# Pairs 2 and 3 get their stacked halves of x from ScalarE and VectorE; the table's scaling moves to GpSimd; new order up to pair 5

## The chip, the cores and the metric

One NeuronCore of a Trainium2 chip runs the kernel. Its engines are TensorE (PE; PEld is its weight load), VectorE (DVE), ScalarE (ACT), GpSimd (POOL) and SyncE (SP), which only issues DMAs here. The metric is the device time of one execution in microseconds, the median over runs.

## The reference

`x` is (64, 64, 1024) float32: 64 batches of 64 channels by 1024. Each batch picks one of 16 weight matrices of 64 by 64, and what comes out goes through a 1024 by 1024 linear layer whose weights are packed 6-bit integers:

```python
W = weights[condition]                      # (64, 64, 64)
h = jnp.einsum('bct,bcd->bdt', x, W)
w = (unpacked.astype(jnp.float32) - zero_point) * scale   # 6-bit fields of qweight
y = jnp.einsum('bsk,nk->bsn', h, w) + bias
return x + y
```

## The kernel before

The 64 batches are worked on as 32 pairs, two pairs to a group (g = p // 2). A pair's x lies on 128 partitions: batch one's channels on the lower 64 (`LO`), batch two's on the upper 64 (`HI`).

**Arithmetic.** PE multiplies in float16, so each float32 operand is cut into a high and a low half. For x, `magnitudes` (ScalarE) sums absolute values, `bounds` (one tiny matmul) spreads the sums, `scales` or `scales_in_full` (DVE) make powers of two of them, `split_1` (ScalarE) writes the scaled high half `hf` and the sums of x, and `split_2` (DVE) the low half `lf`. Stage 1 needs a batch's high half and low half stacked on 128 partitions as one operand `xa`; `stack_high` and `stack_low` do that with four DMAs on SP's queue.

**Stage 1** (`stage1`): 32 matmuls of 64 columns make `ph`, 1024 columns in PSUM, one buffer for all pairs; `stage1_high` (ScalarE) and `stage1_low` (DVE) cut it into `hh` and `hl`. **Stage 2** (`products`): 8 tiles of the contraction, `hh` and `hl`, two PSUM banks: 32 matmuls of 512 columns into `po`, of which even and odd pairs have one buffer each. `stage2_bank(p, n)` is one bank of a pair, `stage2_tiles` some tiles of both.

**Output.** `po` is scaled on DVE (`scale_out`), x is added (`accumulate`) and stored. What the zero points and the bias add has been put onto x by GpSimd (`zero_points`, `add_bias`). For pairs 0 to 3 the result is kept as `res` (`early_minus`, `early_res`) and put onto x later (`early_add`).

**The weights' table** is scaled (`weights_scaled`), cut into halves (`weights_high`, `weights_low`), and each pair's two matrices are selected from it: by GpSimd copies for pairs 2 to 7, by DMAs on SP from pair 8 on. Pairs 0 and 1 take another way: `early_stage1` multiplies x in float32 with unscaled weights, and `early_bounds`, `early_scales`, `early_high`, `early_low` cut the result.

**Order.** The order of instructions on each engine is the order in which the code is written; nothing reorders it. Each engine runs its own list and waits on semaphores, so an instruction that waits holds up all behind it on its engine, and the same holds for DMAs on SP. Up to pair 3 the steps stand one by one (L540 to L678); from pair 3 on `window(p)` issues stage 1 of pair p + 1, the tails of pair p - 1, the preparation of the next groups, and stage 2 of pair p. A run of dummy matmuls (`WARM`) comes first.

Of the kernel before, what the change touches and what calls it, by code (L numbers as in the profile page):

```python
# [8 lines left out]
F32 = mybir.dt.float32  # L9
# [20 lines left out]
def adaln_ffn(ctx: ExitStack, tc: tile.TileContext, x, cond, cw, qw, ws, wz, bias, out):  # L30
# [6 lines left out]
    NG = NP // 2  # L37
    KT = T // P
    LO, HI = slice(0, C), slice(C, P)
    WARM = 36  # L40

    xf = x.rearrange("(i j) c t -> (j c) i t", j=2)
    of = out.rearrange("(i j) c t -> (j c) i t", j=2)
# [6 lines left out]
    unpacking = ExitStack()  # L50
    qp = unpacking.enter_context(tc.tile_pool(name="qp", bufs=3))
    ps_s = ctx.enter_context(tc.tile_pool(name="ps_s", bufs=2, space=bass.MemoryType.PSUM))
    ps_o = [ctx.enter_context(tc.tile_pool(name="ps_a", bufs=1, space=bass.MemoryType.PSUM))]

    ctx.enter_context(tc.manual_schedule())
    ctx.enter_context(nc.allow_low_precision("bounds of magnitudes alone"))
# [10 lines left out]
    def load_x(g):  # L67
        xts[g] = xp.tile([P, 2, T], F32, name="xt")
        nc.sync.dma_start(xts[g], xf[:, 2 * g : 2 * g + 2, :])
# [26 lines left out]
    load_pair(3)  # L96
    nc.sync.dma_start(scb, ws.rearrange("n o -> (n o)").partition_broadcast(P))
    load_x(2)


    dummy = const.tile([P, P], BF, name="dummy")
# [79 lines left out]
        powers(tmp["pw"], wup, wdn)  # L181

    def weights_scaled():
        nc.vector.tensor_tensor(wsc, w32, wdn.unsqueeze(2).to_broadcast([P, NK, D]), ALU.mult)

    def weights_high():
        nc.scalar.copy(tab[:, :, 0, :], wsc)
# [100 lines left out]
    def split_2(g, i, ts_=ALL):  # L288

        nc.vector.scalar_tensor_tensor(  # L290
            st[g]["lf"][:, i, ts_],
            xts[g][:, i, ts_],
            st[g]["down"][:, i : i + 1],
            st[g]["hf"][:, i, ts_],
            ALU.mult,
            ALU.subtract,
        )

    def stack_high(g, sl=BOTH, ts_=ALL):
# [84 lines left out]
    def early_bounds(p, parts):  # L384
        pl = ps_s.tile([P, 2], F32, name="pl", tag="s")
        for n in range(parts):
            nc.tensor.matmul(pl, lhsT=all_ones, rhs=pb[:, p, n, :], start=(n == 0), stop=(n == parts - 1))
        tmp["pl"] = pl
# [8 lines left out]
    def early_stage1(p, ph, kts=range(KT)):  # L397
        for kt in kts:
            nc.tensor.matmul(  # L399
                ph[:, kt % ph.shape[1], :, :], lhsT=xts[0][:, p, ts(kt, P)], rhs=wbd[:, p, :], start=True, stop=True  # L400
            )
# [50 lines left out]

    def stage1(p):
        g, i = divmod(p, 2)
        ph = ps_o[2].tile([P, KT, 2, D], F32, name="ph")
        for kt in range(KT):
            for j in range(2):
                for a in range(2):
                    nc.tensor.matmul(  # L459
                        ph[:, kt, j, :],  # L460
                        lhsT=st[g]["xa"][:, i, j, ts(kt, P)],
                        rhs=wsts[g][:, i, a, j, :],
                        start=(a == 0),
                        stop=(a == 1),
                    )
        return ph.rearrange("p k j d -> p k (j d)")
# [25 lines left out]

    def stage2_tiles(p, kts, ks=range(2)):
        if p not in pos:
            pos[p] = ps_o[p % 2].tile([P, N], F32, name="po", tag="po")
        products(pos[p], p, kts, ks, BANKS, BANKS)

    def stage2_bank(p, n, ks=range(2), kts=range(KT)):
        if p not in pos:
            pos[p] = ps_o[p % 2].tile([P, N], F32, name="po", tag="po")  # L500
        for k in ks:
            products(pos[p], p, kts, [k], [BANKS[n]], [BANKS[n]])

# [40 lines left out]
    early = ExitStack()  # L544
    ps_e = early.enter_context(tc.tile_pool(name="ps_e", bufs=2, space=bass.MemoryType.PSUM))
    ph0a, ph0b = [ps_e.tile([P, KT // 2, 2, D], F32, name="ph0") for _ in range(2)]
    ph1 = ps_e.tile([P, KT, 2, D], F32, name="ph1", bufs=1)
    HALF = [slice(0, T // 2), slice(T // 2, T)]
    early_select(0, 0, nc.gpsimd)
    early_select(0, 1, nc.scalar)  # L550
# [9 lines left out]
    early_rows(0, 0)  # L560
    early_rows(0, 1)
    early_stage1(0, ph0b, range(4, KT))
    early_bounds(0, 2)
    early_scales(0)
    early_high(0, ph0a, LOWER)
    early_high(0, ph0b, UPPER)
    early_weights(1)
    early_stage1(1, ph1)
    unpack(0)
    unpack(1)  # L570
    early_low(0, ph0a, LOWER)
# [8 lines left out]
    early_rows(1, 0)  # L580
    unpack(6, 2)
    early_sums(0)
    stage2_tiles(0, range(2, 4))
    weights_bounds()
    early_bounds(1, 1)
# [2 lines left out]
    weights_scaled()  # L588
    magnitudes(1, 0)
    early_high(1, ph1, slice(0, KT))  # L590
    stage2_tiles(0, range(4, 5))
    bounds(1, FIRST)
    scales(1, FIRST)
    stage2_tiles(0, range(5, 6))
    early_low(1, ph1, slice(0, KT))
    early.close()
    for n in ("b", "h"):
        ps_o.append(ctx.enter_context(tc.tile_pool(name="ps_" + n, bufs=1, space=bass.MemoryType.PSUM)))
    split_1(1, 0)
    stack_high(1, FIRST)  # L600
    weights_high()
    split_2(1, 0)
    stack_low(1, FIRST)
    load_pair(6)
    stage2_tiles(0, range(6, KT))
    early_feature_sums(0)
    weights_low()
    early_unscales(0)
    unpacking.close()
    late = ctx.enter_context(tc.tile_pool(name="late", bufs=1))  # L610
    for n in range(2, 8):
        select_pair(n, nc.gpsimd)
    magnitudes(1, 1)


    stage2_tiles(1, range(0, 4), [0])
    early_zero_points(0)
    stage2_tiles(1, range(0, 4), [1])
    bounds(1, SECOND)
    scales(1, SECOND)  # L620
    early_out(0)
    early_sums(1)
    split_1(1, 1)
    stack_high(1, SECOND)
    split_2(1, 1)
    stack_low(1, SECOND)
    load_pair(7)
    nc.sync.dma_start(bib, bias.partition_broadcast(P))
    stage2_tiles(1, range(4, 7))
    ph = stage1(2)  # L630
    magnitudes(2, 0)
    stage1_high(2, ph, LOWER)
    stage1_high(2, ph, UPPER)
    magnitudes(2, 1)
    stage2_tiles(1, range(7, KT))
    stage1_low(2, ph)
    early_unscales(1)
    weights_hot()


    stage2_bank(2, 0, [0])
    bounds(2)
    scales(2)
    sums_high(1)
    sums_low(1, nc.gpsimd)
    split_1(2, 0)
    stage2_bank(2, 0, [1], range(0, 6))
    weights_of_batches()
    stage2_bank(2, 0, [1], range(6, KT))
    early_feature_sums(1)  # L650
    early_zero_points(1)
    unscales(1)
    unscales(2)
    split_2(2, 0)
    stack_high(2, FIRST)
    stack_low(2, FIRST)
    feature_sums(1)
    unscale_sums(1)
    early_minus(1)
    ph = stage1(3)  # L660
    stage1_high(3, ph)
    stage1_low(3, ph)
    early_res(1)
    split_1(2, 1)
    sums_high(2)
    magnitudes(3, 0)
    magnitudes(3, 1)
    early_zero_points(2)
    stage2_bank(2, 1)
    sums_low(2, nc.vector)  # L670
    split_2(2, 1)
    stack_high(2, SECOND)
    stack_low(2, SECOND)
    nc.vector.tensor_tensor(zsc, zsb, scb, ALU.mult)
    load_x(4)
    early_zero_points(3)
    add_bias(4)
    add_bias(5)  # L678


    LATE = {5 + 2 * n: ((add_bias, early_add)[n % 2], n // 2) for n in range(8)}
# [1 line left out]
    def window(p):  # L683

        g, i = divmod(p, 2)
        if p + 1 < NP:
            ph = stage1(p + 1)
        if p == 3:

            stage2_bank(p, 0)  # L690
        if i == 1 and g + 2 < NG:
            bounds(g + 2)
        if i == 1 and g + 1 < NG:
            feature_sums(g + 1)
        if p - 1 < 4:
            early_out(p - 1)
        else:
            scale_out(p - 1)
        if i == 1 and g + 2 < NG:
            scales_in_full(g + 2)  # L700
        if i == 1 and g + 1 < NG:
            unscale_sums(g + 1)
        if p + 1 < NP:
            stage1_high(p + 1, ph)
        if p - 1 >= 4:
            accumulate(p - 1)
            store(p - 1)
        if p + 1 < NP:
            stage1_low(p + 1, ph)
        if i == 0:  # L710
            if g + 3 < NG:
                load_x(g + 3)
            if g + 1 < NG:
                sums_high(g + 1)
                sums_low(g + 1, nc.scalar)
            if g + 2 < NG:
                magnitudes(g + 2, 0)
                magnitudes(g + 2, 1)
            if g + 1 < NG:
                add_bias(p + 2)  # L720
                add_bias(p + 3)
            if g + 2 < NG:
                select(g + 2)
        else:
            if g + 2 < NG:
                for n in range(2):
                    split_1(g + 2, n)
                    split_2(g + 2, n)
                stack_high(g + 2)
                stack_low(g + 2)  # L730
            if g + 1 < NG:
                zero_points(p + 1)
                zero_points(p + 2)
        if p in LATE:

            what, n = LATE[p]
            what(n)
            if what is early_add:
                store(n)
        if p == 3:  # L740
            stage2_bank(p, 1)
        elif p < NP - 1:
            stage2(p)
# [2 lines left out]
        window(p)  # L746

    p = NP - 1
    for cols, pool, tag in ((slice(0, 512), ps_o[1], "po"), (slice(512, 768), ps_o[2], "ph"), (slice(768, N), ps_o[0], "po")):
        po = pool.tile([P, cols.stop - cols.start], F32, name="pe", tag=tag)  # L750
        products(po, p, range(KT), range(2), [cols], [slice(0, cols.stop - cols.start)])
        scale_out(p, cols, po)
        accumulate(p, cols, po)
        store(p, cols)
# [61 lines left out]
```

## Time and profile before

| what | us |
|---|---|
| median of three runs | 270.55 (270.04 to 270.96) |
| the profiled execution | 271.06 |
| its span | 269.3 |
| PE busy | 261.7 (97%) |
| DVE busy | 199.8 (74%) |
| POOL busy | 168.8 (63%) |
| ACT busy | 158.3 (59%) |
| DMA queue, share of 16 engines' span | 66.9% |
| granted PE clock | 0.999 |

"Span" is the time from the profile's first instruction to its last; the execution's own time is 1.8 us longer. In lines of a timeline the columns are start and duration in us, engine, source line, operation, the tiles written and read, partitions of each operand by shape, and the count; in square brackets stands how long the engine was idle before it and what ended that. In lines of the chain they are start, duration, and what the time went to; "issue" is time without a visible cause, "SPq" SP's issuing of a DMA. A line of the waits names the engine and line that waited, what for, the total in us, the times, and the longest. A matmul's duration overlaps the next one's, so its starts are more telling than its ends.

### The profile page before, as it was taken

To read this page: it belongs to the slowest core of one execution; us is meant where nothing else is said; L and a number is where in the kernel's file an instruction comes from. 1 tells how busy PE (TensorE), PEld (TensorE's weight loads), DVE (VectorE), ACT (ScalarE), POOL (GpSimd) and SP (SyncE) were. 2 spreads that over 40 slices of the span, in tenths; PEclk is the share of its full clock that TensorE was granted. 3 is DMA by queue.
4 is the path that set the end of the run, shared out by engine and by line. 5 is a ranking of instruction groups with operands and counts; after the bars stand their busy time and mean duration, and the time that the engine had idled before them with its cause. 6 is when DMAs were issued, how large, how long until landed. Compare 5 with 4: busy or idle time off the path is not lost.

```text
span 269.3 us, 5717 instructions
## 1 busy us (share of the span) xinstructions
PE 261.7 (97%) x2154; PEld 140.4 (52%) x2154; DVE 199.8 (74%) x271; ACT 158.3 (59%) x283; POOL 168.8 (63%) x96
## 2 busy tenths in 40 slices
PE   8999979999999999999999999999999999999993
PEld 7645535545555554555555455555455555545553
DVE  3897899585795959779595976959598695955543
ACT  3588888576655657666565765656676555634100
POOL 3004253949598695959969596995929386595100
PEclk9999999999999999999999999999999999999999
DMA  6997766957567696597956797677976764551112
GB/s 192 326 356 182 235 133 203 259 167 214 198 148 246 198 266 218 141 322 199 290 170 192 219 268 235 181 245 230 279 222 185 210 170 142 161 158 79 78 50 108
DMA packets 32476, 54.39 MB, mean 202 GB/s; under 512 B 15168, under 2 KB 15424, under 8 KB 32448
## 3 DMA queue, kind: packets, MB, share of 16 engines
q1 hardware_dynamic: 32416, 54.01, 66.9%
q8 instruction: 17, 0.28, 0.4%
q14 instruction: 11, 0.09, 0.1%
q10 hardware_dynamic: 32, 0.00, 0.0%
HBM read 19.93 MB, written 16.78 MB: 136 GB/s over the span
## 4 chain that ended last, share of the span: by engine, by line
PE 89%; DMA 6%; DVE 3%; issue 1%; SPq 1%; DVEq 0%
PE po L483 75%; PE ph L459 10%; DMA xa<-lf 3%; PE pe L483 3%; DMA xt<-in_x_dram 2%; DVE lf L290 1%; PE ph L399 1%; DVE po L432 0%; PE pu L330 0%; SPq L65 0%; DVE hl L475 0%; SPq L307 0%; SPq L86 0%; DVE hs L341 0%; DVE pe L524 0%
## 5 line engine op out<-in xcount | busy, mean ns | idle before, releaser
L483 PE MATMUL po<-q,hl 128*128 128x512 f16 x496 | 118.7, 379 | 0.0
L483 PE MATMUL po<-q,hh 128*128 128x512 f16 x496 | 118.4, 379 | 0.0
L519 POOL TENSOR_TENSOR xt<-xt,zt 128x1024 f32<-128x1024 f32 x28 | 78.7, 2831 | 52.4 <-ACT zt L517 52.4
L483 PEld LDWEIGHTS <-hl 128*128 128x128 f16 x520 | 50.7, 98 | 59.2
L512 POOL TENSOR_TENSOR xt<-xt,bib 128x1024 f32<-128x1024 f32 x32 | 75.4, 2377 | 6.9 <-DVE hs L341 3.9
L471 ACT CAST hh<-ph 128x1024 f16<-128x1024 f32 (+1 forms) x31 | 30.4, 982 | 80.5 <-PE ph L459 42.5
L483 PEld LDWEIGHTS <-hh 128*128 128x128 f16 x520 | 48.3, 98 | 51.8 <-ACT hh L471 0.3
L524 DVE SCALAR_TENSOR_TENSOR po<-po,u,scb 128x1024 f32<-128x1024 f32 x27 | 34.8, 1287 | 52.2 <-PE po L483 52.2
L290 DVE SCALAR_TENSOR_TENSOR lf<-xt,down,hf 128x1024 f16<-128x1024 f32 x30 | 60.3, 2047 | 0.0
L459 PEld LDWEIGHTS <-xa 128*128 128x128 f16 x960 | 32.2, 98 | 9.2 <-issue 2.4
L475 DVE TENSOR_TENSOR hl<-ph,hh 128x1024 f16<-128x1024 f32 x30 | 36.5, 1215 | 0.6 <-ACT hh L471 0.6
L280 ACT ACTIVATE hf<-xt,down 128x1024 f16<-128x1024 f32 x30 | 34.2, 1144 | 4.0 <-DVE down L133 3.9
L459 PE MATMUL ph<-wst,xa 128*128 128x64 f16 x960 | 33.4, 193 | 1.8 <-DMA xa<-lf 1.8
L529 DVE TENSOR_TENSOR xt<-po,xt 128x1024 f32<-128x1024 f32 x27 | 33.1, 1225 | 1.9
L256 ACT ACTIVATE junk<-xt 128x1024 bf16<-128x1024 f32 x30 | 31.7, 1057 | 2.5 <-DMA xt<-in_x_dram 1.7
L517 ACT ACTIVATE zt<-zsc,hs 128x1024 f32<-128x1024 f32 x28 | 30.5, 1138 | 0.0
L323 ACT ACTIVATE xh<-xh,xs 64x1 f16<-64x1 f16 x52 | 12.4, 287 | 0.5
L232 POOL COPY wst<-tab 128x128 f16 x12 | 2.9, 287 | 14.2 <-DVE tab L190 14.2
L448 POOL TENSOR_TENSOR xt<-xt,res 128x1024 f32<-128x1024 f32 x4 | 9.4, 2360 | 0.0
L483 PE MATMUL pe<-q,hh 128*128 128x256 f16 (+1 forms) x24 | 6.6, 308 | 0.0
L483 PE MATMUL pe<-q,hl 128*128 128x256 f16 (+1 forms) x24 | 6.5, 308 | 0.0
L313 ACT CAST xh<-xs 64x2 f16<-64x2 f32 x30 | 5.8, 192 | 0.4
(86 smaller groups left out, 104.9 us busy)
## 6 DMA issues: line engine op xcount, KB each, us to landing
out_dram<-xt SPq DMA_DIRECT2D x31, 512.0 KB, 3.0
xt<-in_x_dram SPq DMA_DIRECT2D x13, 1024.0 KB, 7.2
xa<-hf SPq DMA_DIRECT2D x26, 256.0 KB, 3.8
xa<-lf SPq DMA_DIRECT2D x26, 256.0 KB, 3.8
xt<-in_x_dram SPq DMA_DIRECT2D x5, 512.0 KB, 5.9
wst<-tab SPq DMA_DIRECT2D x48, 32.0 KB, 3.1
xa<-hf SPq DMA_DIRECT2D x8, 128.0 KB, 3.2
xa<-lf SPq DMA_DIRECT2D x8, 128.0 KB, 2.7
```

Of the source, the lines that this page charges most:

```text
L256: nc.scalar.activation(junk, xts[g][:, i, :], AF.Abs, accum_out=st[g]["l1"][:, i : i + 1])
L280: nc.scalar.activation(st[g]["hf"][:, i, ts_], xts[g][:, i, ts_], AF.Copy, scale=st[g]["down"][:, i : i + 1], accum_out=st[g]["xs"][:, i : ...
L290: nc.vector.scalar_tensor_tensor(st[g]["lf"][:, i, ts_], xts[g][:, i, ts_], st[g]["down"][:, i : i + 1], st[g]["hf"][:, i, ts_], ALU.mult, ...
L459: nc.tensor.matmul(ph[:, kt, j, :], lhsT=st[g]["xa"][:, i, j, ts(kt, P)], rhs=wsts[g][:, i, a, j, :], start=(a == 0), stop=(a == 1),)
L471: nc.scalar.copy(hs_pair[p][0][:, kts, :], ph[:, kts, :])
L475: nc.vector.tensor_tensor(hl[:, kts, :], ph[:, kts, :], hh[:, kts, :], ALU.subtract)
L483: nc.tensor.matmul(po[:, a], lhsT=hs_pair[p][k][:, kt, :], rhs=qT[:, kt, c], start=(kt == 0 and k == 0), stop=(kt == KT - 1 and k == 1),)
L512: nc.gpsimd.tensor_tensor(xt, xt, bib, ALU.add)
L517: nc.scalar.activation(zt, zsc, AF.Copy, scale=st[g]["hs"][:, i : i + 1])
L519: nc.gpsimd.tensor_tensor(xt, xt, zt, ALU.subtract)
L524: nc.vector.scalar_tensor_tensor(po, po, st[g]["u"][:, i : i + 1], scb[:, cols], ALU.mult, ALU.mult)
L529: nc.vector.tensor_tensor(xts[g][:, i, cols], po, xts[g][:, i, cols], ALU.add)
```

## The change

Pairs 2 and 3 (group 1) no longer use `hf`, `lf` and DMAs: `stacked_high` lets ScalarE write each batch's scaled high half straight into `xa`, 64 partitions at a time, and `stacked_low` lets DVE write the low half to the other 64 partitions. `weights_scaled` goes from DVE to GpSimd, and so does the product of zero points and scales, `zsc`, which now stands between the selections of pairs 3 and 4. x of pairs 6 and 7 and the bias are loaded among the first loads. There are 40 dummies in place of 36. Stage 1's PSUM buffer is opened at the start and holds pair 1's float32 result too. Two of eight tiles of pair 1's float32 stage 1 stand in front of `early_bounds(0)`. In the steps up to pair 3 much is moved: both pairs' early sums, unscales and feature sums stand together, `weights_hot` comes before pair 0's output and pair 2's stage 1, and both splits of group 2 follow stage 1 of pair 3. In window 3 bank 0 of pair 3 comes ahead of stage 1 of pair 4.

```diff
-    WARM = 36
+    WARM = 40
...
     load_x(2)
+    load_x(3)
+    nc.sync.dma_start(bib, bias.partition_broadcast(P))
...
-        nc.vector.tensor_tensor(wsc, w32, wdn.unsqueeze(2).to_broadcast([P, NK, D]), ALU.mult)
+        nc.gpsimd.tensor_tensor(wsc, w32, wdn.unsqueeze(2).to_broadcast([P, NK, D]), ALU.mult)
...
+    HALVES_OF = ((LO, HI), (HI, LO))
+    def stacked_high(g, i):
+        s = slice(i, i + 1)
+        for j, (h, _) in enumerate(HALVES_OF):
+            nc.scalar.activation(
+                st[g]["xa"][h, i, j], xts[g][h, i], AF.Copy, scale=st[g]["down"][h, s], accum_out=st[g]["xs"][h, s]
+            )
+    def stacked_low(g, i, j):
+        h, o = HALVES_OF[j]
+        xa = st[g]["xa"]
+        nc.vector.scalar_tensor_tensor(
+            xa[o, i, j], xts[g][h, i], st[g]["down"][h, i : i + 1], xa[h, i, j], ALU.mult, ALU.subtract
+        )
...
-    ph1 = ps_e.tile([P, KT, 2, D], F32, name="ph1", bufs=1)
+    ph1 = ps_o[0].tile([P, KT, 2, D], F32, name="ph")
...
     early_stage1(0, ph0b, range(4, KT))
+    early_stage1(1, ph1, range(0, 2))
     early_bounds(0, 2)
...
-    early_stage1(1, ph1)
+    early_stage1(1, ph1, range(2, KT))
...
     early_sums(0)
+    early_sums(1)
...
-    split_1(1, 0)
-    stack_high(1, FIRST)
+    stacked_high(1, 0)
+    for j in range(2):
+        stacked_low(1, 0, j)
     weights_high()
-    split_2(1, 0)
-    stack_low(1, FIRST)
-    load_pair(6)
     stage2_tiles(0, range(6, KT))
     early_feature_sums(0)
+    early_feature_sums(1)
+    magnitudes(1, 1)
+    early_zero_points(0)
     weights_low()
-    early_unscales(0)
...
-    for n in range(2, 8):
+    for n in range(2, 4):
         select_pair(n, nc.gpsimd)
-    magnitudes(1, 1)
+    nc.gpsimd.tensor_tensor(zsc, zsb, scb, ALU.mult)
+    for n in range(4, 8):
+        select_pair(n, nc.gpsimd)
     stage2_tiles(1, range(0, 4), [0])
-    early_zero_points(0)
     stage2_tiles(1, range(0, 4), [1])
     bounds(1, SECOND)
     scales(1, SECOND)
-    early_out(0)
-    early_sums(1)
-    split_1(1, 1)
-    stack_high(1, SECOND)
-    split_2(1, 1)
-    stack_low(1, SECOND)
-    load_pair(7)
-    nc.sync.dma_start(bib, bias.partition_broadcast(P))
+    early_unscales(0)
+    early_unscales(1)
+    weights_hot()
+    early_minus(0)
+    early_res(0)
     stage2_tiles(1, range(4, 7))
+    stacked_high(1, 1)
+    stacked_low(1, 1, 0)
     ph = stage1(2)
-    magnitudes(2, 0)
     stage1_high(2, ph, LOWER)
     stage1_high(2, ph, UPPER)
+    early_zero_points(1)
+    stage2_tiles(1, range(7, KT))
+    magnitudes(2, 0)
     magnitudes(2, 1)
-    stage2_tiles(1, range(7, KT))
     stage1_low(2, ph)
-    early_unscales(1)
-    weights_hot()
+    stacked_low(1, 1, 1)
+    weights_of_batches()
+    unscales(1)
...
```

After that the steps stand in this order, up to the windows:

```python
sums_high(1); sums_low(1, nc.gpsimd); early_minus(1)
stage2_bank(2, 0)
ph = stage1(3); stage1_high(3, ph)
bounds(2); feature_sums(1); scales(2); unscales(2); unscale_sums(1); early_res(1)
split_1(2, 0); stack_high(2, FIRST); split_2(2, 0); stack_low(2, FIRST)
split_1(2, 1); stack_high(2, SECOND)
stage1_low(3, ph)
stage2_bank(2, 1)
split_2(2, 1); stack_low(2, SECOND)
sums_high(2); sums_low(2, nc.gpsimd); early_zero_points(2)
magnitudes(3, 0); magnitudes(3, 1)
load_x(4); add_bias(5); add_bias(4); early_zero_points(3)
```

In `window(3)`, `stage2_bank(p, 0)` stands before `stage1(p + 1)`, where it stood after it.

More of the change, by code (lines that the diff above doesn't have):

```diff
@@ L52, in adaln_ffn @@
     ps_s = ctx.enter_context(tc.tile_pool(name="ps_s", bufs=2, space=bass.MemoryType.PSUM))
-    ps_o = [ctx.enter_context(tc.tile_pool(name="ps_a", bufs=1, space=bass.MemoryType.PSUM))]
+    ps_o = [ctx.enter_context(tc.tile_pool(name="ps_" + n, bufs=1, space=bass.MemoryType.PSUM)) for n in ("h", "a")]
     ctx.enter_context(tc.manual_schedule())
@@ L454, in stage1 @@
         g, i = divmod(p, 2)
-        ph = ps_o[2].tile([P, KT, 2, D], F32, name="ph")
+        ph = ps_o[0].tile([P, KT, 2, D], F32, name="ph")
         for kt in range(KT):
@@ L494, in stage2_tiles @@
         if p not in pos:
-            pos[p] = ps_o[p % 2].tile([P, N], F32, name="po", tag="po")
+            pos[p] = ps_o[1 + p % 2].tile([P, N], F32, name="po", tag="po")
         products(pos[p], p, kts, ks, BANKS, BANKS)
@@ L499, in stage2_bank @@
         if p not in pos:
-            pos[p] = ps_o[p % 2].tile([P, N], F32, name="po", tag="po")
+            pos[p] = ps_o[1 + p % 2].tile([P, N], F32, name="po", tag="po")
         for k in ks:
@@ L590, in adaln_ffn @@
     early_high(1, ph1, slice(0, KT))
-    stage2_tiles(0, range(4, 5))
+    stage2_tiles(0, range(4, 6))
     bounds(1, FIRST)
     scales(1, FIRST)
-    stage2_tiles(0, range(5, 6))
     early_low(1, ph1, slice(0, KT))
     early.close()
-    for n in ("b", "h"):
-        ps_o.append(ctx.enter_context(tc.tile_pool(name="ps_" + n, bufs=1, space=bass.MemoryType.PSUM)))
-    split_1(1, 0)
-    stack_high(1, FIRST)
+    ps_o.append(ctx.enter_context(tc.tile_pool(name="ps_b", bufs=1, space=bass.MemoryType.PSUM)))
+    stacked_high(1, 0)
+    for j in range(2):
+        stacked_low(1, 0, j)
     weights_high()
-    split_2(1, 0)
-    stack_low(1, FIRST)
-    load_pair(6)
     stage2_tiles(0, range(6, KT))
     early_feature_sums(0)
+    early_feature_sums(1)
+    magnitudes(1, 1)
+    early_zero_points(0)
     weights_low()
-    early_unscales(0)
     unpacking.close()
     late = ctx.enter_context(tc.tile_pool(name="late", bufs=1))
-    for n in range(2, 8):
+    for n in range(2, 4):
         select_pair(n, nc.gpsimd)
-    magnitudes(1, 1)
+    nc.gpsimd.tensor_tensor(zsc, zsb, scb, ALU.mult)
+    for n in range(4, 8):
+        select_pair(n, nc.gpsimd)
     stage2_tiles(1, range(0, 4), [0])
-    early_zero_points(0)
     stage2_tiles(1, range(0, 4), [1])
@@ L620, in adaln_ffn @@
     scales(1, SECOND)
-    early_out(0)
-    early_sums(1)
-    split_1(1, 1)
-    stack_high(1, SECOND)
-    split_2(1, 1)
-    stack_low(1, SECOND)
-    load_pair(7)
-    nc.sync.dma_start(bib, bias.partition_broadcast(P))
+    early_unscales(0)
[3 more added lines that the diff above has]
+    early_res(0)
     stage2_tiles(1, range(4, 7))
+    stacked_high(1, 1)
+    stacked_low(1, 1, 0)
     ph = stage1(2)
-    magnitudes(2, 0)
     stage1_high(2, ph, LOWER)
     stage1_high(2, ph, UPPER)
+    early_zero_points(1)
+    stage2_tiles(1, range(7, KT))
+    magnitudes(2, 0)
     magnitudes(2, 1)
-    stage2_tiles(1, range(7, KT))
     stage1_low(2, ph)
-    early_unscales(1)
-    weights_hot()
-    stage2_bank(2, 0, [0])
-    bounds(2)
-    scales(2)
+    stacked_low(1, 1, 1)
+    weights_of_batches()
+    unscales(1)
     sums_high(1)
     sums_low(1, nc.gpsimd)
[L646 to L658, printed above, removed]
     early_minus(1)
+    stage2_bank(2, 0)
     ph = stage1(3)
     stage1_high(3, ph)
+    bounds(2)
+    feature_sums(1)
+    scales(2)
+    unscales(2)
+    unscale_sums(1)
+    early_res(1)
+    split_1(2, 0)
+    stack_high(2, FIRST)
+    split_2(2, 0)
+    stack_low(2, FIRST)
+    split_1(2, 1)
+    stack_high(2, SECOND)
     stage1_low(3, ph)
-    early_res(1)
-    split_1(2, 1)
+    stage2_bank(2, 1)
+    split_2(2, 1)
+    stack_low(2, SECOND)
     sums_high(2)
+    sums_low(2, nc.gpsimd)
+    early_zero_points(2)
     magnitudes(3, 0)
     magnitudes(3, 1)
[L668 to L674, printed above, removed]
     load_x(4)
+    add_bias(5)
+    add_bias(4)
     early_zero_points(3)
-    add_bias(4)
-    add_bias(5)
     LATE = {5 + 2 * n: ((add_bias, early_add)[n % 2], n // 2) for n in range(8)}
@@ L685, in window @@
         g, i = divmod(p, 2)
+        if p == 3:
+            stage2_bank(p, 0)
         if p + 1 < NP:
             ph = stage1(p + 1)
-        if p == 3:
-            stage2_bank(p, 0)
         if i == 1 and g + 2 < NG:
@@ L748, in adaln_ffn @@
     p = NP - 1
-    for cols, pool, tag in ((slice(0, 512), ps_o[1], "po"), (slice(512, 768), ps_o[2], "ph"), (slice(768, N), ps_o[0], "po")):
+    for cols, pool, tag in ((slice(0, 512), ps_o[2], "po"), (slice(512, 768), ps_o[0], "ph"), (slice(768, N), ps_o[1], "po")):
         po = pool.tile([P, cols.stop - cols.start], F32, name="pe", tag=tag)
```

## The prediction

> **What bounds the kernel now.** First the chain that ended last: PE holds 89% of it, and from 53.85 us on it is one unbroken repetition (53.85 to 69.66, then 15.81 us for every two pairs) until the last store. The change touches nothing behind window 5, so only what PE loses before about 53 us can move the end. Then the waits of the first 62 us on PE, and its timeline.
>
> ```profile
> PE ph L459 <- DMA xa<-lf: 1.8, 3, 1.2
> PE ph L399 <- DMA xt<-in_x_dram: 0.6, 2, 0.4
> ```
> ```profile
> 31.12 1.89 PE L483 MATMUL po<-q,hh 128*128 128x512 f16 x8
> 32.84 1.89 PE L483 MATMUL po<-q,hl 128*128 128x512 f16 x8
> 35.21 0.22 PE L459 MATMUL ph<-wst,xa 128*128 128x64 f16 x2 [0.47 <-DMA xa<-lf]
> 36.58 1.04 PE L459 MATMUL ph<-wst,xa 128*128 128x64 f16 x30 [1.15 <-DMA xa<-lf]
> 37.45 1.89 PE L483 MATMUL po<-q,hh 128*128 128x512 f16 x8
> ...
> 52.32 0.22 PE L459 MATMUL ph<-wst,xa 128*128 128x64 f16 x2
> 52.71 1.03 PE L459 MATMUL ph<-wst,xa 128*128 128x64 f16 x30 [0.17 <-DMA xa<-lf]
> 53.58 0.17 PE L260 MATMUL pl<-l,ones 128*128 128x2 bf16 x1
> ```
>
> Matmul ends are modelled, so I count from start to start. Eight 512-column matmuls are 1.73 us apart (0.216 each), the 32 of stage 1 take 0.93 in the steady part. The batch started at 32.84 should have been followed at 34.57, and the next batch at 35.50; it came at 37.45: 1.95 us lost before stage1(4). Before stage1(6), 52.32 to 53.58 is 1.26 for 0.93: 0.33 lost. Those 2.3 us, with some 0.2 at a bounds matmul near 15.3, are the most that a new order can win: 268.1 from the median.
>
> What feeds the second of those waits:
>
> ```profile
> 43.18 2.48 DVE lf L290 x2
> 45.66 0.02 issue
> 45.68 0.59 SPq L307
> 46.27 0.04 issue
> 46.31 6.26 DMA xa<-lf
> 52.58 0.14 issue
> ```
> The four stacking DMAs of group 3 (1 MB) go out from 43.94 (hf) to 46.31 and the last lands at 52.58: 8.64 us after the first issue.
>
> **The change, part by part.** All durations are start-to-start from the rows of before; "after" times are my own sums.
>
> *Nothing on the path.* Four more dummies: 36 take 4.02 us, so four take 0.45; PE then waits 0.40 us for the second half of pair 0 anyway. Were that cover gone they would cost 0.45. load_x(3) and the bias go to the queue's head, behind load_x(2): the first loads land in order of issue (9.6 to 13.1 us after it), so those in front keep their times; x of pairs 6, 7 is read first near 36 us. load_pair(6), load_pair(7) leave SP where the stacking stood. The shared PSUM buffer makes stage1(2) wait for early_low(1), done by 18.1, used at 24.2. early_sums(1) earlier: ScalarE stood idle 1.72 us before 14.10, which hides its 1.18. Table's scaling and zsc leave DVE (1.23 us each).
>
> *Early part.* Two tiles of early_stage1(1) now stand in front of early_bounds(0), so that matmul waits for pair 1's x (8.48): 8.48 + 4 x 0.116 = 8.94 where it was 8.13. DVE's powers move from 8.40 to 9.20, and everything behind them by 0.8. PE reaches stage 2 at 10.44 (10.34 before) and the low half of tiles 0 to 3 comes at 11.5 where PE asks at 11.44: 0.1 lost. Further on there is slack: PE passes bounds(1, SECOND) at 21.55, against 21.50, with both feature sums behind it.
>
> *Scaling on GpSimd.* No such row; the nearest are L512 and L519 (128x1024 f32, two inputs): 2.36 alone, up to 3.38 while DVE also worked on it. From 15.1 it ends at 17.6 to 18.5. ScalarE's weights_high comes to it at 19.0, and bounds(1, SECOND) has 0.4 us more: up to 4.3 us it costs nothing, beyond that PE pays all of it. I take 0. zsc (2.5) sits between the selections of pairs 3 and 4; pair 4's weights are there by 27, needed at 38.
>
> *stacked_high.* Two 64x1024 activations where one 128x1024 stood (L280, 1.15). Half the lanes is either half the work (0.6, as L407's 128x512) or none saved (1.15); L395's 64x1 takes 0.16 like L422's 128x1, so I take 1.15 each. Both pairs then end at 19.0 and 24.6 on ScalarE, before DVE and PE want more of it; the lower end gains nothing.
>
> *stacked_low.* Two 64x1024 on DVE for one L290 at 1.28. Bounds by rows: 0.67 (L414, 128x512) and 2.05 (the mean of L290 in the whole span, 3.38 its longest, both while GpSimd worked). I take 1.28 each, since GpSimd is idle or copying 0.24 us pieces then.
>
> [...]
>
> *The new wait.* DVE is now full from the first stacked_low on. Before, the low half of pair 2 just made it:
>
> ```profile
> 21.74 0.17 DVE L132 TENSOR_SCALAR pl<-pl 128x1 f32<-128x1 f32 x1 [1.23 <-PE pl L260]
> ...
> 22.20 1.29 DVE L432 SCALAR_TENSOR_TENSOR po<-po,u,zt 128x1024 f32<-128x1024 f32 x1
> 23.52 1.22 DVE L438 TENSOR_TENSOR res<-po,scb 128x1024 f32<-128x1024 f32 x1
> 24.66 1.27 DVE L290 SCALAR_TENSOR_TENSOR lf<-xt,down,hf 128x1024 f16<-128x1024 f32 x1
> 26.52 1.23 DVE L475 TENSOR_TENSOR hl<-ph,hh 128x1024 f16<-128x1024 f32 x1 [0.58 <-ACT hh L471]
> ```
> There it ended at 27.75 and PE used it at 27.83. Now four unscales (0.57) and weights_hot (0.76) stand in front: 21.82 + 0.46 + 0.57 + 0.76 + 1.32 + 1.14 + 1.28 + 1.23 = 28.58. PE: 21.58 + 12 x 0.216 + 1.05 (stage1) + 0.87 + 0.13 + 1.73 = 27.95. PE waits 0.65 to 0.7; queued behind are bank 0 of pair 2 and stage1(3), for which ScalarE waits. stage1(3) starts at 30.37 (30.12 before).
>
> *The wait removed at stage1(4).* Bank 0 of pair 3 moves ahead of it: 30.37 + 1.0 + 0.13 + 3.46 + 3.46 = 38.42. split_2 of pair 4 ends at 35.1, SP's second issue stands at 35.65, and landings of such pieces took 2.3 to 3.4: 38.0 to 39.0. Idle DMA queues speak for 2.7 (the median): no wait; up to 0.5 for the range. Stage 1 of pair 4 and bank 0 of pair 3 are then done at 39.4, against 40.9.
>
> *stage1(6).* PE gets there at 39.4 + 3.46 + 0.95 + 0.1 + 6.92 = 50.8. Its operand: ScalarE works without a break from stage1_high(3) at 31.6 (0.9 + 2.29 + 0.41 + 1.09 + 2.36 + 1.09 + 0.9) to 40.65 and splits pairs 6 and 7 until 43.0; it was 43.9. DVE's first split there meets add_bias of GpSimd (0.3), the second ends at 44.7, the last issue is at 45.4. With 6.26 it lands at 51.7, with the 8.64 from the first hf issue (43.1) at 51.7; the steady group issued at 57.09 had its last landing 8.0 after, which gives 51.1. The nearest row is the same group, and my ScalarE sum may be 0.1 to 0.2 long: 51.55, where before it was 52.65 (52.32 + 0.33). PE still waits 0.75 here.
>
> Sum: 1.95 + 0.33 + 0.2 (the early bounds) removed, 0.1 + 0.67 + 0.75 put in their place, which leaves 0.96; the landing argument gives 52.65 - 51.55 = 1.1. I take 1.05. The profiled execution took 271.06 with a span of 269.3, 0.5 above the median of the three runs; taking the same off the median: 270.55 - 1.05 = 269.5.
>
> **The rivals.**
> - *The group's DMAs land in time* (5.0 us, as the last of the steady group's, rather than 6.26). PE's own sum, 50.8, holds, and only the wait for pair 2's low half is left: 1.85 saved, 268.7. For: lighter DMA traffic once no pair-2 and pair-3 stacking runs. Against: load_x(5) still follows at once.
> - *The gain is eaten.* Landing of pair 4 at 3.3 instead of 2.7 and each stacked instruction some 0.2 longer: 0.45 at stage1(4), 0.4 at pair 2's low half, of which 0.75 passes on to ScalarE's chain and the landing: 0.3 saved, 270.2.
> - *Slower: stacked_low runs against GpSimd.* At 2.05 each, three stand in front of pair 2's low half: 3 x 0.77 = 2.3 later, PE waits 3.0 there, stage1(6) is at 53.9: 1.3 lost, 271.8. It decides (0.8 us lost) from 1.9 each. For: L290's mean. Against: scaling should be over when the first starts, and only copies run beside the third.
> - *The change doesn't do what it says*: the order of instructions in the built program has the new operations in place and no stacking transfer for pairs 2 and 3; I give this nothing of its own.
>
> **How the numbers follow.** 0.42 for 269.5 (its own range 269.1 to 269.9), 0.22 for 268.7, 0.18 for eaten, 0.18 for slower. About 0.3% (0.8 us, so below 269.74 and above 271.36) is what a measurement of this kernel can tell from no change. Faster: 0.22 and most of the 0.42 (0.33): 0.55. Slower: 0.18 and a little of the tail of the eaten case: 0.19. Within: the rest, 0.26. The range takes in the first three cases with their ends, 268.5 to 270.7, and leaves out the slower one.
>
> **What would show it.** Right: no stacking DMA of 128 KB before 33 us; a PE gap of 0.5 to 0.9 us near 28 released by hl; none over 0.5 before stage1(4) near 38.4; a gap before stage1(6), its matmuls at 51.1 to 51.9; then 15.8 us for every two pairs. Wrong: stacked_low far from 1.28; a gap at bounds(1, SECOND) near 21.6 (scaling too slow); no gap near 28; the steady part no longer 15.8.

## The result and the profile after

The changed kernel took 272.29 us, the median of five runs (271.85 to 273.08). Five runs of the kernel before had a median of 270.13 (269.81 to 270.96). The ratio is 1.0079, with a 95% interval of 1.0052 to 1.0105: slower by 0.8%, where 0.4% faster was forecast.

The two profiled executions differ by less, 271.85 against 271.06 (spans 270.1 and 269.3). The profiled one is the fastest of the five runs of after, and the first loads landed earlier in it (the load of x issued at 2.48 that its chain waited for took 5.07 us, before 5.87): PE passes the bounds matmul of pair 1's second half, bounds(1, SECOND), at 20.90, where before it was 21.50. So I count from that matmul.

The chain that ended last holds less DMA than before, 2% where it was 6%, by engine:

```profile
PE 94%; DMA 2%; DVE 1%; SPq 1%; ACT 0%; issue 0%
```

PE's waits in the first 62 us (total, times, longest). The stacking transfers that led this list before are gone, and a wait of 2.3 us for VectorE stands at its head:

```profile
PE po L503 <- DVE res L458: 2.3, 1, 2.3
PE pc L562 <- DVE one L106: 1.1, 1, 1.1
PE ph L419 <- DMA xt<-in_x_dram: 0.8, 2, 0.5
```

PE's timeline around it and at the two places where it waited before (L503 is stage 2, L479 stage 1; start, duration, what):

```profile
20.90 0.17 PE L262 MATMUL pl<-l,ones 128*128 128x1 bf16 x1
...
25.40 0.20 PE L209 MATMUL pb__625<-hot,up_w 16*128 16x64 bf16 x1
27.92 3.41 PE L503 MATMUL po<-q,hh 128*128 128x512 f16 x8 [2.31 <-DVE res L458]
31.16 1.89 PE L503 MATMUL po<-q,hl 128*128 128x512 f16 x8
32.89 1.10 PE L479 MATMUL ph<-wst,xa 128*128 128x64 f16 x32
...
39.13 1.89 PE L503 MATMUL po<-q,hl 128*128 128x512 f16 x8
40.86 1.10 PE L479 MATMUL ph<-wst,xa 128*128 128x64 f16 x32
...
53.21 1.26 PE L479 MATMUL ph<-wst,xa 128*128 128x64 f16 x32
54.31 0.17 PE L262 MATMUL pl<-l,ones 128*128 128x2 bf16 x1
...
54.44 1.89 PE L503 MATMUL po<-q,hh 128*128 128x512 f16 x8
```
The same places in the kernel before (bounds(1, SECOND), stage1(3), the batch behind stage1(6)):

```profile
21.50 0.17 PE L260 MATMUL pl<-l,ones 128*128 128x1 bf16 x1
...
30.12 1.16 PE L459 MATMUL ph<-wst,xa 128*128 128x64 f16 x32
...
53.71 1.89 PE L483 MATMUL po<-q,hh 128*128 128x512 f16 x8
```

stage1(4) starts at 40.86 without a wait. stage1(6) starts on time at 53.21 but takes 1.10 to the next row, 0.17 over PE's own 0.93, where before it lost 0.33. So nearly all that the change was to remove is removed. But the eight matmuls at 27.92 come 2.31 us late and take 3.24 us to the next batch instead of 1.73. From bounds(1, SECOND) to stage1(3) it is now 32.89 - 20.90 = 11.99, where it was 30.12 - 21.50 = 8.62: 3.37 lost. To the batch behind stage1(6) (54.44, before 53.71) it is 33.54 against 32.21, so 2.04 of that is won back behind stage1(3), nearly all of it by the removed waits, and 1.33 stays lost.

Why was res late? VectorE's timeline:

```profile
22.32 0.24 DVE L197 TENSOR_SCALAR hot<-cb,kio 16x64 bf16<-16x64 int32 x1
22.48 2.34 DVE L199 TENSOR_TENSOR up_k<-wup,eye 16x16 f32<-16x16 f32 x1
24.86 0.16 DVE L201 TENSOR_REDUCE up<-up_k 16x1 f32<-16x16 f32 x1
25.06 0.26 DVE L203 TENSOR_SCALAR up_w<-spread,up 16x128 bf16<-16x128 bf16 x1
25.24 1.27 DVE L452 SCALAR_TENSOR_TENSOR po<-po,u,zt 128x1024 f32<-128x1024 f32 x1
26.55 1.23 DVE L458 TENSOR_TENSOR res<-po,scb 128x1024 f32<-128x1024 f32 x1
```
The same stretch on GpSimd:

```profile
21.49 0.99 POOL L234 COPY wst<-tab 128x128 f16 x4 [5.14 <-DVE tab L192]
22.45 2.35 POOL L633 TENSOR_TENSOR zsc<-zsb,scb 128x1024 f32<-128x1024 f32 x1
24.75 1.95 POOL L234 COPY wst<-tab 128x128 f16 x8
```

The product up_k of 16x16 elements took 0.16 in the kernel before:

```profile
28.19 0.16 DVE L197 TENSOR_TENSOR up_k<-wup,eye 16x16 f32<-16x16 f32 x1
```
Here it lasts 2.34, and it ends with GpSimd's zsc, which started 0.03 us ahead of it. It is the second step of weights_hot, behind which res stands.

And why did the eight matmuls crawl? Windows on PE, the first of 2 us, the others of 0.2 (length, busy time and count, granted clock, DMA share, GB/s):

```profile
25.40:27.40 2.00, 0.20 (x2) 1.00 0.02 4
27.60:27.80 0.20, 0.00 (x0) 0.56 0.00 0
27.80:28.00 0.20, 0.08 (x1) 0.50 0.17 41
30.80:31.00 0.20, 0.20 (x2) 0.50 0.00 0
31.00:31.20 0.20, 0.20 (x3) 0.91 0.00 0
31.20:31.40 0.20, 0.20 (x3) 1.00 0.00 0
```

PE's last matmul ended at 25.60. Some 2 us later, in the window from 27.60 and just before work came, the granted clock fell to 0.50, and it was back in the window from 31.00: 3.4 us.

### The profile page after: what moved, and what is told of

Same layout as the page of the kernel before. It is cut to its first block, busy times and chain, and to the rows that moved or that the text cites. A ratio compares the mean times of both kernels' runs of the same rounds, so it can differ in the third digit from the quotient of the medians.

```text
span 270.1 us, 5703 instructions
## 1 busy us (share of the span) xinstructions
PE 261.8 (97%) x2158; PEld 139.9 (52%) x2158; DVE 204.1 (76%) x269; ACT 161.2 (60%) x287; POOL 172.2 (64%) x100
## 4 chain that ended last, share of the span: by engine, by line
PE 94%; DMA 2%; DVE 1%; SPq 1%; ACT 0%; issue 0%
PE po L503 80%; PE ph L479 10%; PE pe L503 3%; DMA xt<-in_x_dram 2%; PE ph L419 1%; PE pu L350 1%; DVE po L452 0%; DVE res L458 0%; SPq L65 0%; SPq L86 0%; ACT hh L491 0%; DVE pe L544 0%; DVE xt L549 0%; PE pu L441 0%; PE pl L407 0%
## 5 line engine op out<-in xcount | busy, mean ns | idle before, releaser
L503 PE MATMUL po<-q,hh 128*128 128x512 f16 x496 | 120.0, 382 | 2.3 <-DVE res L458 2.3
L503 PE MATMUL po<-q,hl 128*128 128x512 f16 x496 | 118.5, 379 | 0.0
L503 PEld LDWEIGHTS <-hl 128*128 128x128 f16 x520 | 50.8, 98 | 59.8 <-issue 0.4
L503 PEld LDWEIGHTS <-hh 128*128 128x128 f16 x520 | 48.7, 98 | 54.9 <-ACT zt L447 2.4
L532 POOL TENSOR_TENSOR xt<-xt,bib 128x1024 f32<-128x1024 f32 x32 | 74.5, 2355 | 1.9 <-issue 1.9
L479 PEld LDWEIGHTS <-xa 128*128 128x128 f16 x960 | 32.2, 98 | 7.2
L479 PE MATMUL ph<-wst,xa 128*128 128x64 f16 x960 | 33.0, 193 | 0.0
L282 ACT ACTIVATE hf<-xt,down 128x1024 f16<-128x1024 f32 x28 | 31.9, 1143 | 0.0
L339 POOL TENSOR_TENSOR xh<-xs,xh 64x2 f16<-64x2 f32 x4 | 0.8, 194 | 10.7 <-ACT xh L333 10.6
L186 POOL TENSOR_TENSOR wsc<-w,wdn 128x1024 f32<-128x1024 f32 x1 | 1.9, 1902 | 8.3 <-DVE wup L138 8.3
L503 PE MATMUL pe<-q,hh 128*128 128x256 f16 (+1 forms) x24 | 6.6, 308 | 0.0
L503 PE MATMUL pe<-q,hl 128*128 128x256 f16 (+1 forms) x24 | 6.5, 308 | 0.0
```

The lines of the kernel that those rows point to most:

```text
L282: nc.scalar.activation(st[g]["hf"][:, i, ts_], xts[g][:, i, ts_], AF.Copy, scale=st[g]["down"][:, i : i + 1], accum_out=st[g]["xs"][:, i : ...
L479: nc.tensor.matmul(ph[:, kt, j, :], lhsT=st[g]["xa"][:, i, j, ts(kt, P)], rhs=wsts[g][:, i, a, j, :], start=(a == 0), stop=(a == 1),)
L503: nc.tensor.matmul(po[:, a], lhsT=hs_pair[p][k][:, kt, :], rhs=qT[:, kt, c], start=(kt == 0 and k == 0), stop=(kt == KT - 1 and k == 1),)
L532: nc.gpsimd.tensor_tensor(xt, xt, bib, ALU.add)
```

## The experiments

Each was run beside the kernel before; ratios to it have 95% intervals. "Bounds to stage 1" is the stretch used above: 8.62 before, 11.99 after.

**Let GpSimd make up_k itself, ahead of zsc**

```diff
-nc.vector.tensor_tensor(up_k, wup[0:NK, :], eye[0:NK, 0:NK], ALU.mult)
...
+nc.gpsimd.tensor_tensor(tmp["up_k"], wup[0:NK, :], eye[0:NK, 0:NK], ALU.mult)
 nc.gpsimd.tensor_tensor(zsc, zsb, scb, ALU.mult)
```

> Only the 16x16 product up_k (line 199 of the changed kernel) moves: GpSimd makes it between the selection of pair 3 and zsc, so DVE has no operation with two SBUF operands while zsc runs. Theory A (the product took 2.34 us because it was kept out until GpSimd's zsc had ended): DVE's weights_hot is back at some 0.7 us, res of pair 0 comes 2.1 us earlier, PE's wait ahead of bank 0 of pair 2 falls from 2.31 to about 0.5, too short for the clock to fall, so those eight matmuls are 1.73 us apart again instead of 3.24; a wait of about 0.7 for the low half of pair 2 takes its place. Stage 1 of pair 3 starts 9.3 us after bounds(1, SECOND), where the changed kernel has 12.0: 2.7 us gained, 269.6. Theory B (DVE is late for what was put in front of it as a whole, and the product is long for a reason of its own): the wait stays near 2.3 and the time at 272.3.

274.60 us (273.08 to 275.81), ratio 1.0154 [1.0102, 1.0206]: a miss, by its median slower than after. VectorE's timeline:

```profile
23.43 0.16 DVE L200 TENSOR_REDUCE up<-up_k 16x1 f32<-16x16 f32 x1
23.62 4.02 DVE L202 TENSOR_SCALAR up_w<-spread,up 16x128 bf16<-16x128 bf16 x1
```
GpSimd's timeline in the same kernel:

```profile
23.36 2.35 POOL L634 TENSOR_TENSOR zsc<-zsb,scb 128x1024 f32<-128x1024 f32 x1
25.66 1.93 POOL L233 COPY wst<-tab 128x128 f16 x8
```

The reduction passes beside zsc in 0.16. The next step, up_w, is held instead, and for longer: to 27.64, when zsc and the eight copies behind it have ended. So it is not up_k as such: with one victim removed, a later instruction of the same chain took the wait.

**Keep PE busy through the wait**

```diff
+pc2 = ps_s.tile([P, P], F32, name="pc2", tag="s")
+for _ in range(36):
+    nc.tensor.matmul(pc2, lhsT=dummy, rhs=dummy, start=True, stop=True)
 stage2_bank(2, 0)
```

> 36 dummy matmuls of 128 columns stand on PE ahead of bank 0 of pair 2, that is inside its wait of 2.31 us (some 2.0 us of work at full clock). Theory A (the wait makes the granted clock fall to 0.50, and that costs a second time): the clock stays at 1.00, the eight matmuls behind the wait are 1.73 us apart, and the end of that batch comes 1.5 us earlier; the low half of pair 2, which DVE has ready at 30.3, then holds PE for 0.7, so that 0.75 us are gained: 271.5. Theory B (these matmuls are slow for another reason, such as their operands): 3.2 us for the eight as before and 272.3.

271.12 us (270.55 to 272.69), ratio 1.0045 [1.0023, 1.0067]. PE's timeline:

```profile
25.93 2.18 PE L668 MATMUL pc<-dummy 128*128 128x128 bf16 x36
28.31 1.89 PE L503 MATMUL po<-q,hh 128*128 128x512 f16 x8 [0.19 <-DVE res L458]
30.79 1.90 PE L503 MATMUL po<-q,hl 128*128 128x512 f16 x8 [0.59 <-DVE hl L495]
```

No row is slow now, and bounds to stage 1 is 32.52 - 21.29 = 11.23. The slow clock had cost 3.24 - 1.73 = 1.51, but 0.75 of it (30.79 - 28.31 less 1.73) covered the wait for hl, the low half, which shows itself here. Net 0.76 in the trace; the two ratios differ by 0.34%, or 0.9 us, though their intervals just overlap. The larger part of the loss, the wait behind res, stays.

**weights_hot early, in VectorE's idle stretch** (called the early version below): zsc stays on GpSimd. weights_hot stands inside weights_powers, behind wup and ahead of wdn, so the table's scaling, which needs wdn, starts behind it; nothing else moves.

```diff
-    powers(tmp["pw"], wup, wdn)
+    sums = tmp["pw"]
...
+    nc.vector.tensor_scalar(wup.bitcast(I32), sums.bitcast(I32), EXPONENT, None, ALU.bitwise_and)
+    weights_hot()
...
     early_unscales(1)
-    weights_hot()
```

> weights_hot as a whole goes to where DVE stood idle for 1.2 us, inside weights_powers and ahead of wdn, so that neither GpSimd's scaling nor zsc runs beside it; zsc stays on GpSimd. Theory A: res of pair 0 is ready before PE gets there, no wait ahead of bank 0 of pair 2 and no fall of the clock; the low half of pair 2 comes 0.1 to 0.3 late. Stage 1 of pair 3 starts 8.1 to 8.4 us after bounds(1, SECOND), 3.6 to 3.9 less than in the changed kernel. What PE gains beyond some 2.5 us may be held again at stage 1 of pair 6 by the stacking DMAs: 268.5 to 269.7. Theory B (the lateness comes from the two-half instructions and the output of pair 0): at most weights_hot's planned 0.76 us gained, 271.5.

268.33 us (267.79 to 268.84), ratio 0.9933 [0.9906, 0.9960]: faster than both. up_k takes its 0.16 again, at 15.03, ahead of GpSimd's scaling, and PE's timeline has one small gap left:

```profile
26.18 1.90 PE L509 MATMUL po<-q,hh 128*128 128x512 f16 x8
28.30 1.90 PE L509 MATMUL po<-q,hl 128*128 128x512 f16 x8 [0.22 <-DVE hl L501]
30.04 1.10 PE L485 MATMUL ph<-wst,xa 128*128 128x64 f16 x32
```

Bounds to stage 1 is 8.50, a little over the 8.1 to 8.4 expected, and the time a little better than the range. All other parts of the change are in this kernel, so they are worth more than their cost, and the place of weights_hot turned the sign.

**Only zsc back on VectorE** (behind split_2 of pair 5), all else as in after:

```diff
-nc.gpsimd.tensor_tensor(zsc, zsb, scb, ALU.mult)
...
 split_2(2, 1)
 stack_low(2, SECOND)
+nc.vector.tensor_tensor(zsc, zsb, scb, ALU.mult)
```

> The changed kernel with only the product zsc back on DVE, where it stood in the kernel before, behind split_2 of pair 5; order and all else as changed. Theory A (GpSimd's zsc keeps DVE out): weights_hot takes 0.7 to 0.8 with the 16x16 product at 0.16, PE waits some 0.4 ahead of bank 0 of pair 2 and 0.7 for its low half, the clock stays at 1.00, stage 1 of pair 3 starts 9.2 us after bounds(1, SECOND) against 12.0. DVE's 1.2 us at their old place may come back in part at stage 1 of pair 6: 269.5 to 270.2. Theory B (it was the selections' copies, or the order alone): the long wait stays, 272.

269.66 us (268.92 to 270.24), ratio 0.9972 [0.9936, 1.0007]. PE's timeline:

```profile
25.97 1.89 PE L503 MATMUL po<-q,hh 128*128 128x512 f16 x8 [0.23 <-ACT hh L491]
28.45 1.90 PE L503 MATMUL po<-q,hl 128*128 128x512 f16 x8 [0.59 <-DVE hl L495]
30.19 1.10 PE L479 MATMUL ph<-wst,xa 128*128 128x64 f16 x32
```

weights_hot stands where the change put it, up_k takes 0.25, no batch of eight is slow (1.89 and 1.90), and bounds to stage 1 is 9.16. This is the kernel nearest to the one that my sum described: a wait for hl alone (0.75 start to start, 0.67 worked out) and 0.30 at the batch before it (25.97 less the 0.13 behind the matmul at 25.54). Its median is within 0.2 us of the forecast, in part by luck: at stage1(6) it loses 0.20 (50.92 to 52.05, for 0.93) where the sum kept 0.75, but it also loses that 0.30 and 0.35 ahead of stage1(5) (40.94 to 43.02, for 1.73), which the sum did not have.

**Only the direct stacking, in the kernel before** (in short, for both pairs i; the first pair's high and low halves have weights_high between them)

```diff
-split_1(1, i); stack_high(1, i); split_2(1, i); stack_low(1, i)
+stacked_high(1, i)
+stacked_low(1, i, 0); stacked_low(1, i, 1)
```

> The kernel before with stacked_high and stacked_low for pairs 2 and 3 in the places of the splits and their DMAs, and nothing else changed. Theory A (the direct stacking costs only DVE's and ScalarE's added instructions, 1.25 us each): the two more on DVE stand ahead of pair 2's low half, which just made it in the kernel before, so PE waits there for about 1.2 us, and the waits for pair 4's operand and pair 6's stay: 270.1 plus 1.2 is 271.3. Theory B (64-partition instructions that write to the other half are themselves slow, near the 2.05 us of L290's mean): 3 us or more lost. If the direct stacking is a gain by itself: below 269.3.

270.62 us (269.82 to 271.87), ratio 1.0018 [0.9990, 1.0047]: no difference, and 0.7 below what I expected. The wait that it adds is ScalarE's, not VectorE's:

```profile
26.50 1.90 PE L501 MATMUL po<-q,hh 128*128 128x512 f16 x8 [1.27 <-ACT hh L489]
```

In the old order two stacked halves for one split put ScalarE 1.27 late. At stage1(4) 0.93 is lost where it was 1.95, and at stage1(6) nothing, which pays it back. By itself the stacking gains nothing here; the new order without the stacking was not run, so how the gain of the early version divides between them is open.

**The early version with pair 1's unscales later, and with the table's scaling back on VectorE**

```diff
 # first kernel: early version, with
-early_unscales(1)
...
 stacked_low(1, 1, 1)
+early_unscales(1)
 # second kernel: early version, with
-nc.gpsimd.tensor_tensor(wsc, ...)
+nc.vector.tensor_tensor(wsc, ...)
```

> The run with weights_hot moved early (268.33), and also early_unscales(1), two instructions of 0.16 us, taken out from in front of pair 0's output to behind the last half of pair 3. Theory A: the 0.22 us that PE still waited for the low half of pair 2 go, 268.1; nothing else changes. If DVE's order there is no longer what holds PE: 268.3, with the wait at another operand.

268.53 us (267.81 to 269.51), ratio 0.9929 [0.9896, 0.9962]. The 0.22 wait is gone (8.10 from bounds to stage 1, which is PE's own work), and the time is that of the early version: a gain of 0.2 is below what these runs can tell.

> The run with weights_hot moved early, and the table's scaling back on DVE (the part of the change that was taken to cost and win nothing). DVE's 1.23 us follow at 15.6 where bounds(1, FIRST) is asked for at 16.2, so everything behind them on DVE moves by some 0.6; the two-half instructions of pair 2 then start 0.6 later, weights_low with them, and pair 2's low half comes 0.5 to 0.6 later: 268.9. If GpSimd's scaling hurt (it ended late or held up DVE), this one is faster: below 268.

269.42 us (268.72 to 269.83), ratio 0.9958 [0.9927, 0.9990]. Its first-62-us waits on PE, of which the stacking's 0.6 and ScalarE's 0.3 are not in the early version:

```profile
PE ph L485 <- DMA xa<-lf: 0.6, 1, 0.6
PE pl L268 <- ACT junk L264: 0.3, 1, 0.3
PE po L509 <- DVE hl L501: 0.3, 1, 0.3
```

So the scaling on GpSimd, which I had at nothing, points to a gain: 0.9 us against the kernel above it, from the same chip, which also has the unscales moved, and 0.25% by the ratios to the early version itself. The intervals overlap, so neither the gain nor its size is firm.

**Two probes**: the early version with trials behind its last store. In each, GpSimd multiplies 128x1024 by 128x1024 and then copies, and one small instruction of VectorE starts during the product. Their whole times (313.19 and 305.36) include the trials and are not compared.

```diff
+nc.gpsimd.tensor_tensor(big, zsb, scb, ALU.mult)
+for _ in range(8):
+    nc.gpsimd.tensor_copy(few, tab[:, 3, :, :])
 # VectorE beside it, one per trial:
+nc.vector.tensor_tensor(o1, wup[0:NK, :], src2, ALU.mult)
+nc.vector.tensor_scalar(o2, spread, late_sum[:, 0:1], None, ALU.mult)
+nc.vector.tensor_reduce(o3, src2, AX.X, ALU.add)
+nc.vector.tensor_tensor(o4, pq[0:NK, 0:NK], src2, ALU.mult)
...
```

> The kernel with weights_hot moved early, and behind its last store a string of trials that add time: in each, GpSimd does a 128x1024 product and eight 128x128 copies back to back, and DVE, some 0.6 us after the start, one small instruction: two SBUF operands (float32 16x16), a bfloat16 16x128 times a pointer scalar, a reduction, one PSUM and one SBUF operand, float32 times a constant, an integer comparison, and the first two again. [...] The second, by the run with the product on GpSimd, also waits for all eight copies (3.5 us or more), the first only for the product (about 1.8). Theory B (any small DVE instruction is kept out, or it is chance): no difference between the forms, or between a form's two trials.

```profile
266.12 2.07 DVE L794 TENSOR_TENSOR o<-wup,src 16x16 f32<-16x16 f32 x1
271.76 2.09 DVE L797 TENSOR_SCALAR o<-spread,late_sum 16x128 bf16<-16x128 bf16 x1
277.41 0.15 DVE L800 TENSOR_REDUCE o<-src 16x1 f32<-16x16 f32 x1
283.18 0.16 DVE L803 TENSOR_TENSOR o<-pq,src 16x16 f32<-16x16 f32 x1
288.70 2.07 DVE L806 TENSOR_SCALAR o<-src 16x16 f32<-16x16 f32 x1
294.34 2.09 DVE L809 TENSOR_SCALAR o<-cb,kio 16x64 bf16<-16x64 int32 x1
```

The product of the first trial ran from 265.83 to 268.17, and the instruction ended at 268.19; so in each of the held forms. Held are two inputs in SBUF, and the three scalar forms; let through are the reduction and the product with one input in PSUM. None waited for the copies. In the second probe each copy goes to a tile of its own, so that they are 0.24 us apart as in the kernel, and the last trials have copies alone or two products alone:

> The first probe again, but with GpSimd's copies going to eight different tiles, so that they follow each other without a gap as the selections do (0.24 us apart; in the first probe 0.35, each waiting for the one before to the same tile). What is open is why up_w, a bfloat16 instruction with a pointer scalar, waited 4.0 us, through zsc and all eight selections, in the run with the product on GpSimd. [...] Theory B (only the instruction that runs first counts): all forms 1.8 to 2.1 with the product, under 0.5 with copies alone, and the 4.0 us stay unexplained.

Beside product and copies it was 2.07 to 2.09 again; beside 16 copies alone 0.24 and 0.26; beside two products 2.09, so it got in after the first:

```profile
293.81 0.26 DVE L798 TENSOR_SCALAR o<-spread,late_sum 16x128 bf16<-16x128 bf16 x1
298.19 2.09 DVE L798 TENSOR_SCALAR o<-spread,late_sum 16x128 bf16<-16x128 bf16 x1
```
In these probes an instruction waits for the GpSimd instruction that is running, and no longer. Why up_w in the first experiment waited for the copies too is not reproduced by this and stays open.

## Why the prediction was wrong, point by point

**The step that failed** is under "Scaling on GpSimd": "zsc (2.5) sits between the selections of pairs 3 and 4", costed by its own length on GpSimd and by what GpSimd does next. I looked at what waits for zsc and not at what runs beside it. The term it spoils is weights_hot, 0.76 in the sum, which measured 25.24 - 22.32 = 2.92.

**The bill closes.** PE's own work from bounds to stage 1 is 8.10. The predicted wait for hl measured 0.75 and the gap at the batch before it 0.30, which gives 9.15 (9.16 measured with zsc on VectorE). zsc on GpSimd makes that gap 2.38 by start times (28.31 - 25.80 - 0.13 in the kernel with dummies; 2.39 in after), 2.08 more, and the clock adds 0.76 net: 11.99, as measured. These 2.84 us, on the forecast gain of 1.05, make a loss of 1.8; the five runs had 2.2, with an interval of 1.4 to 2.8. That the last step comes so near is in part luck: the forecast gain had a wait of 0.75 at stage1(6) that measured 0.17, and it did not have the 0.30.

**The clock** was in no part of my sum, though a wait on PE was. A wait is not only its length, if the clock falls in it: here 2.31 us, and 1.51 more in the slow matmuls behind it.

**The waits removed** were right: stage1(4) starts without one. stage1(6) was better than I had it: 0.17 lost, where I kept 0.75. The last of group 3's transfers landed in 5.3 instead of 6.26, which is the first rival's mechanism. In the early version PE, there at 50.36, lost nothing. It is not safely gone: in its first 62 us PE waited 0.2 for such a transfer with the unscales later, and 0.6 with the table's scaling on VectorE.

**The wait added** at hl was sized well (0.67 taken, 0.75 measured with zsc on VectorE), but in after it is covered by the slow clock.

**Costs by nearest rows**: stacked_high 1.27 a piece with its accumulator read (1.15 taken, of the activation alone), stacked_low 1.26 to 1.31 start to start (1.28 taken), zsc 2.35 (2.5), the scaling 1.90 (2.4 to 3.4) and off the path as taken. No size here was the fault. The steady part kept its 15.8.

**The rivals.** My slower one had the right pair of engines, VectorE against GpSimd, and, by coincidence, nearly the right time (271.8), but the wrong place: it took stacked_low as the one that suffers, which held its 1.28. I looked for contention only where a row of before had already shown it, in large instructions. In the early version, where copies do run beside a stacked_low, that one is 1.42 and the copies take 2.93 instead of 1.95: small for VectorE.

## What to carry to other kernels

Before work goes to GpSimd, list what VectorE executes during it, the small instructions first: a 16x16 product of 0.16 us paid all that was left of a 128x1024 one (2.34), and everything behind it did too. Put a chain of small steps where GpSimd is idle (here into a stretch that VectorE had free anyway), rather than moving its steps one by one. Count a new wait on PE once by its length and, if it is long enough for the clock to fall (2.3 us here, not 1.3), once more by the slow matmuls behind it.

## What the runs showed of the hardware

With a GpSimd product of 128x1024 from SBUF running, a small VectorE instruction that started behind it and had two inputs in SBUF, or was one of the three scalar forms tried, lasted until that product ended: 2.07 to 2.09 us in the probes, 2.34 for up_k in the changed kernel. A reduction and a product with one input in PSUM did not (0.15 and 0.16). The rows show how little the size of the held instruction mattered: forms of 16x16, 16x64 and 16x128 all took 2.07 to 2.09, and up_k, 0.16 before, became some fifteen times as long. The 4.02 us of up_w in the first experiment, through nine GpSimd instructions, are more than the probes give.

A gap of 2.31 us on PE was enough for half the clock in the changed kernel: it fell 2 us after the last matmul and stayed at 0.50 for 3.4. Through the gap of 1.15 us ahead of stage1(4) in the kernel before it stayed at 1.00, and behind one of 1.27, with direct stacking alone, the eight matmuls took 1.74 us to the next row, which is full speed. When it falls is not fixed by the gap alone: in the first experiment, behind gaps of 1.49 and 2.34 us with one short matmul between them, the eight matmuls took 3.09 us to the next batch, and those eight 2.05 to stage 1, each for 1.73. From these two, with half speed while it is slow, I estimate that the clock fell some 0.4 us after PE had begun to work again and was back some 3.4 us later.
